# Order around the v, q and k products, weights loaded and combined in order of use, and the last projection in plain products

## The chip, the cores and the metric

The kernel runs on one core of one Trainium2 chip. The metric is device time in microseconds (us) of one execution; lower is better. Every run below was in the fast state, with a mean granted TensorE clock of 0.991 to 0.997 of full speed, so runs can be compared directly. "Span" is the time from the first to the last instruction in the profiled execution; it is about 1.8 us shorter than the timed run.

Engines are named as in the profile: PE is TensorE, PEld its weight loads, DVE is VectorE, ACT is ScalarE, POOL is GpSimd, SP is SyncE, which issues most transfers.

## The reference, cut to what matters

B = 32 batches, N = 512 nodes, D = 512 features, float32, one 0/1 adjacency matrix for all batches.

```python
# layer 0: graph step with residual and layer norm
deg = adj.sum(axis=1)
y   = deg[None, :, None] * (x @ Wi.T + b) + einsum('ij,bjo->bio', adj, x @ Wj.T)
h   = layernorm(x + y)
# layer 1: masked attention with 8 heads of 64, residual, layer norm
q, k, v = h @ Wq.T + bq, h @ Wk.T + bk, h @ Wv.T + bv       # split into heads
s   = where(adj == 0, -inf, q @ k.T / sqrt(64))
out = layernorm(h + (softmax(s) @ v) @ Wo.T + bo)
```

## The kernel before

**Seven pieces for one product.** Each 512 x 512 x 512 product of layer 0 (l0, two products in one), of v, q, k and of the output projection (pj) is made of seven half-size products ("pieces") of sums and differences of quarters, which fall into three PSUM groups. The weights' combinations are made once ahead of the loop and stored to HBM; they come back 256 KB at a time through a ring of 12 tiles. The activations' combinations (`combos`) are made by GpSimd for every batch.

```python
GROUP = {1: "X", 2: "X", 6: "Y", 7: "Y", 4: "Y", 5: "Z", 3: "Z"}   # which PSUM group a piece adds to
ORDER = (1, 2, 6, 7, 4, 5, 3)

def mm_tile(bank):                       # two banks, "a" and "b", one buffer each
    return psum.tile([P, 512], FT, name="mm" + bank, bufs=1)
def big():
    return work([P, 4, N], "big", 6)     # six large tiles in rotation

def piece(kind, b, i, bank):
    g = GROUP[i]
    ...                                  # eight matmuls (16 for l0) into the group's bank
    if i == 1:
        nc.scalar.copy(p1, pm)           # ScalarE keeps piece 1; the group goes on in the same bank
    ...                                  # kind v: piece 2 copied by ScalarE, others added by VectorE
    ...                                  # kind q, k: piece 2 emptied by ScalarE, others by VectorE
```

Whatever follows into a bank must wait until the bank is read. The order around v, q and k was:

```python
def phase_c(n):                          # norm[i]: turn 128 normed rows with PE, copy with ScalarE
    res = [norm[0], norm[1], z(apply, n, 1), z(add_bo, n, 0), pc("v", n, 1, "a")]
    ...
    res += [pc("q", n, 1, "b"), pc("v", n, 2, "a"), pc("q", n, 2, "b")]
    ...
    res += [norm[2], z(combos, TH, n, h, (1, 2), 0), pc("k", n, 1, "a"), norm[3], z(combos, TH, n, h, (1, 2), 1),
            z(combos, TH, n, h, (3, 4), 0), z(combos, TH, n, h, (3, 4), 1), z(add_bo, n, 1), pc("k", n, 2, "a")]
    ...
    for i in ORDER[2:]:
        res += [pc("v", n, i, "a"), pc("q", n, i, "b")]
```

**The start.** Six weights are loaded from two queues, and their combinations made, all ahead of the first product. So is the fold of v's bias into the output bias, a small matmul over wo, which stands before the combination of wo.

```python
def combine(name, eng):
    s1, s2, s3, s4, n22 = [ring_tile() for _ in range(5)]
    eng.tensor_tensor(s1, a21, a22, op=OP.add)
    eng.tensor_tensor(s2, s1, a11, op=OP.subtract)
    eng.tensor_tensor(s4, a12, s2, op=OP.subtract)
    eng.tensor_tensor(s3, a11, a21, op=OP.subtract)
    nc.scalar.mul(n22, a22, -1.0)
    ...                                  # seven 256 KB stores to HBM, two of them plain quarters

combine("wj", nc.gpsimd); combine("wi", nc.vector)
...                                      # graph forms: edge, the check of the adjacency (buffer adj_f)
combine("wv", nc.gpsimd); combine("wq", nc.vector); combine("wk", nc.gpsimd)
...                                      # fold: bo_r += bv @ wo
combine("wo", nc.vector)
```

**The loop.** The attention of one batch has eight steps (four head pairs, two halves). Pieces of the neighbouring batches are dealt into the steps, and behind each piece one of the six VectorE steps left over from the head pair (four reciprocal quarters, a check that sums into `told`, the scaling). The last projection runs alone behind the last attention.

## Time and profile before

| | before |
|---|---|
| time, median of 3 runs | 4076.63 us (4075.16 to 4078.4) |
| span of the profiled run | 4072.7 us |
| first l0 product starts | 62.0 us |
| first v piece starts | 88.69 us |
| one batch in the middle | 124.1 us |
| waits of PE between 150 and 3900 us | 109 us |
| from the last sums to the end | 41.1 us |

The prediction shows the totals, the waits and one period. To them belongs the longest of PE's waits in the first 150 us. Columns: who waits for whom, us in total, how often, the longest.

```profile
PE mmb L570 <- DVE big L569: 20.9, 1, 20.9
```

This is the fold (L570), which waits 20.9 us. What is behind it in PE's order waits with it: the rest of the gathering of the first batch begins only at 46.8 us, when the fold is done, and ends at 58.4. The first product then waits 3.6 us more for its weights, whose loads SyncE issues at 58.3, behind the last stores of wo.

### The profile page before, as it was taken

The numbers are of one execution on the slowest core, as the hardware profiler recorded it, in microseconds if no ns is written. First come the engines' busy times: TensorE is split into PE (matmuls) and PEld (weight loads), VectorE is DVE, ScalarE is ACT, GpSimd is POOL, SyncE is SP. The second block draws the span as 40 slices with busy tenths as digits, with TensorE's granted clock in tenths as the row PEclk, the third lists the DMA queues.
The fourth block names the chain that finished last, engine by engine and source line by source line (L and its number), as shares of the span: only waits on it lengthen the run. The fifth ranks groups of instructions, "written<-read, shape, count | busy, mean of one in ns | idle before, by whom it ended". The sixth has DMA issues, their size and how long they took to land.

```text
span 4072.7 us, 47394 instructions
## 1 busy us (share of the span) xinstructions
PE 3878.7 (95%) x17442; PEld 2655.8 (65%) x17442; DVE 2604.5 (64%) x3514; ACT 1058.0 (26%) x1486; POOL 1889.5 (46%) x2010
## 2 busy tenths in 40 slices
PE   6999999999999999999999999999999999999996
PEld 4766666666666666666666666666666666666663
DVE  3576666666666666666666666666666666666665
ACT  2222222222222222222222222222222222222221
POOL 5444544545445445345454454453454444444533
PEclk8999999999999999999999999999999999999998
DMA  8333333233333333332333333333333333333330
GB/s 286 104 99 106 107 111 117 86 114 104 103 120 98 104 106 107 109 118 88 110 109 102 118 99 101 109 109 106 117 98 102 110 103 114 105 95 114 104 101 24
DMA packets 239099, 441.49 MB, mean 108 GB/s; under 512 B 23440, under 2 KB 26512, under 8 KB 238864
## 3 DMA queue, kind: packets, MB, share of 16 engines
q1 hardware_dynamic: 237024, 434.73, 35.4%
q8 instruction: 142, 2.33, 0.2%
q10 hardware_dynamic: 1584, 3.15, 0.2%
q14 instruction: 93, 0.76, 0.1%
q0 software_dynamic: 256, 0.53, 0.0%
HBM read 393.75 MB, written 44.56 MB: 108 GB/s over the span
## 4 chain that ended last, share of the span: by engine, by line
PE 70%; DVE 17%; POOL 6%; issue 3%; ACT 3%; SPq 0%; DMA 0%; POOLq 0%; ACTq 0%; DVEq 0%
PE mma L342 28%; PE mmb L342 15%; PE sc L394 9%; PE ov L416 9%; PE mmb L266 6%; DVE xh L279 5%; DVE rl L429 3%; DVE e L399 3%; POOL big L311 2%; PE ov L423 2%; DVE es L408 2%; POOL mv L235 2%; ACT xh L239 2%; PE sc L259 1%; DVE ov L434 1%
## 5 line engine op out<-in xcount | busy, mean ns | idle before, releaser
L342 PE MATMUL mma<-ring,big 128*128 128x256 f32 x5296 | 1231.1, 382 | 73.3 <-POOL big L311 30.2
L342 PEld LDWEIGHTS mma<-ring,big 128*128 128x128 f32 x5296 | 993.0, 190 | 274.8 <-POOL big L311 41.8
L398 ACT ACTIVATE sc<-sc 128x1024 f32<-128x1024 f32 x512 | 492.9, 1007 | 1645.9 <-PE sc L394 1451.8
L399 DVE TENSOR_TENSOR e<-sc,edge 128x1024 f32<-128x1024 f32 x512 | 602.3, 1218 | 359.3 <-ACT sc L398 359.3
L311 POOL TENSOR_TENSOR big<-big 128x256 f32<-128x256 f32 (+1 forms) x512 | 541.9, 1083 | 289.3 <-DVE big L260 196.7
L405 POOL TENSOR_TENSOR es<-e 128x1024 f32<-128x1024 f32 x128 | 301.2, 2353 | 736.5 <-PE ov L423 699.9
L416 PE MATMUL ov<-e,v 128*64 128x512 f32 x2048 | 500.2, 610 | 26.1 <-DVE told L434 26.1
L394 PE MATMUL sc<-q,k 64*128 64x512 f32 x2048 | 509.6, 616 | 0.4 <-ACT big L288 0.4
L429 DVE RECIPROCAL rl<-ov 128x128 f32<-128x128 f32 x512 | 458.9, 927 | 4.0 <-PE ov L423 0.2
L342 PE MATMUL mma<-big,ring 128*128 128x256 f32 x1792 | 430.2, 383 | 24.2 <-ACT p L349 20.5
L234 POOL TENSOR_SCALAR mv<-mv 128x1 f32<-128x1 f32 x256 | 78.9, 308 | 774.8 <-DVE mv L233 762.0
L342 PE MATMUL mmb<-big,ring 128*128 128x256 f32 x1792 | 432.6, 384 | 0.0
L342 PEld LDWEIGHTS mmb<-big,ring 128*128 128x128 f32 x1792 | 333.1, 190 | 113.9 <-DVE e L399 47.9
L342 PEld LDWEIGHTS mma<-big,ring 128*128 128x128 f32 x1792 | 332.2, 190 | 103.2 <-ACT p L349 27.8
L416 PEld LDWEIGHTS ov<-e,v 128*64 128x64 f32 x2048 | 125.6, 137 | 370.8 <-issue 302.1
L408 DVE TENSOR_TENSOR es<-es,e 128x1024 f32<-128x1024 f32 x256 | 313.4, 1224 | 4.4
L394 PEld LDWEIGHTS sc<-q,k 64*128 64x128 f32 x2048 | 176.4, 186 | 207.8 <-issue 194.8
L360 DVE TENSOR_TENSOR xh<-xh,mma 128x512 f32<-128x512 f32 x192 | 131.7, 686 | 264.5 <-PE mma L342 264.5
L357 POOL TENSOR_TENSOR xh<-xh,p 128x512 f32<-128x512 f32 x192 | 237.9, 1267 | 105.8 <-ACT p L349 105.1
L342 PE MATMUL mmb<-ring,big 128*128 128x256 f32 x1104 | 270.2, 389 | 15.5 <-POOL big L311 15.5
L342 PEld LDWEIGHTS mmb<-ring,big 128*128 128x128 f32 x1104 | 206.6, 192 | 94.9 <-POOL big L311 40.3
L239 ACT ACTIVATE xh<-xh,mv 128x512 f32<-128x512 f32 x256 | 201.8, 813 | 255.5 <-POOL mv L236 255.1
(106 smaller groups left out, 3634.6 us busy)
## 6 DMA issues: line engine op xcount, KB each, us to landing
ring<-wi SPq DMA_DIRECT2D x224, 256.0 KB, 2.6
ring<-wj SPq DMA_DIRECT2D x224, 256.0 KB, 2.7
ring<-wv SPq DMA_DIRECT2D x224, 256.0 KB, 2.6
ring<-wq SPq DMA_DIRECT2D x224, 256.0 KB, 2.6
ring<-wk SPq DMA_DIRECT2D x224, 256.0 KB, 2.7
ring<-wo SPq DMA_DIRECT2D x224, 256.0 KB, 2.6
xh<-in_x_dram SPq DMA_DIRECT2D x32, 1024.0 KB, 5.5
out_dram<-xh SPq DMA_DIRECT2D x32, 1024.0 KB, 5.2
```

Of the source, the lines that this page charges most:

```text
L239: nc.scalar.activation(y, y, AF.Identity, bias=mv[:, 4:5], scale=mv[:, 3:4])
L266: nc.tensor.matmul(pm, parts[w][:, jc, :], adjR[:, jc, :], start=(w == 0 and jc == 0), stop=(w == 1 and jc == NC - 1))
L311: nc.gpsimd.tensor_tensor(dst, p, q, op=OP.subtract)
L342: nc.tensor.matmul(pm[:, c * Q:(c + 1) * Q], lhs, rhs, start=first, stop=(kc == 1 and n == len(terms) - 1), skip_group_check=True)
L357: nc.gpsimd.tensor_tensor(d, d, p1, op=OP.add)
L394: nc.tensor.matmul(ps[:, s, :], KT[b, hp // 2][r, hp % 2, kc * P:(kc + 1) * P], QT[b, hp // 2][r, hp % 2, :], start=True, stop=True)
L398: nc.scalar.activation(ps, ps, AF.Exp)
L399: nc.vector.tensor_tensor(e, ps, edge[:, kc:kc + 1, :].to_broadcast([P, 2, N]), op=OP.mult)
L405: nc.gpsimd.tensor_add(ES[hp], E[0], E[1])
L408: nc.vector.tensor_add(ES[hp], ES[hp], E[kc])
L416: nc.tensor.matmul(PV[hp][s * HD:(s + 1) * HD, :], V[b][:, kc, c0:c0 + HD], E[kc][:, s, :], start=(kc == 0), stop=(kc == NC - 1))
L429: nc.vector.reciprocal(rl[:, c], pl[:, c])
```

## The change

Its intent: fill the hole ahead of the second v piece, deal the leftovers of a head pair faster, start the first product as early as possible by loading and combining the weights in the order of their use, and keep the last projection from running alone. The diff, cut to its core:

```diff
@@ loads: adjacency in four chunks, then x and the weights on one queue @@
-    nc.sync.dma_start(adj_i, rows(adj))
+    for ic in range(NC):
+        nc.sync.dma_start(adj_i[:, ic, :], adj[ic * P:(ic + 1) * P, :])
@@ combine: tiles of a ring of four, two stores fewer @@
-        s1, s2, s3, s4, n22 = [ring_tile() for _ in range(5)]
+        s1, s2, s3, s4, n22 = [t[:, c].rearrange("p (c i) -> p c i", c=2)
+                               for t in [work([P, 2, N], "e", 4) for _ in range(3)] for c in range(2)][:5]
@@ query scale moves from wq into the Exp @@
-        nc.scalar.activation(ps, ps, AF.Exp)
+        nc.scalar.activation(ps, ps, AF.Exp, scale=QSCALE)
@@ phase_a: graph forms while the first batch is gathered @@
+            if n == 0 and i == 3:
+                res += [z(graph_forms)]
@@ phase_b: combinations of wv, wq, wk between the first l0 pieces @@
+                if n == 0:
+                    res += [z(combine, *f) for f in {6: (("wv", nc.vector),), 2: (("wq", nc.vector),),
+                                                     5: (("wk", nc.vector),)}.get(i, ())]
@@ phase_c @@
-        res = [norm[0], norm[1], z(apply, n, 1), z(add_bo, n, 0), pc("v", n, 1, "a")]
+        res = [z(fold)] if n == 0 else []            # fold: combine("wo"), then the bias product
+        res += [norm[0], norm[1], z(apply, n, 1), pc("v", n, 1, "a"), pc("q", n, 1, "b")]
...
-        res += [pc("q", n, 1, "b"), pc("v", n, 2, "a"), pc("q", n, 2, "b")]
...
-        res += [norm[2], z(combos, TH, n, h, (1, 2), 0), pc("k", n, 1, "a"), norm[3], ...
+        res += [norm[2], norm[3], z(combos, TH, n, h, (1, 2)), pc("v", n, 2, "a"), pc("q", n, 2, "b"),
+                pc("k", n, 1, "a"), z(combos, TH, n, h, (3, 4)), z(add_bo, n, 0), z(add_bo, n, 1), pc("k", n, 2, "a")]
@@ leftovers of a head pair: two behind an l0 piece @@
+                    some = ... else max(1, round(f[0] / PC))
@@ last steps: pieces of batch 30 packed two to a step, plain products of batch 31 @@
+        own = [(4 * GA, last_part, hp, 0) for hp in range(3)]
+        return [[z(last_load), p[0], FLUSH] + c, [p[1], p[2]], [p[3], p[4]], [p[5], p[6], z(stats, m, 0), z(stats, m, 1)],
+                [FLUSH, own[0], z(apply, m, 0), z(apply, m, 1), z(store, m)], [own[1]], [FLUSH, own[2]], []]
```

A `last_part(hp, half)` is four plain matmuls of one head pair for two row blocks. Half 0 of the first three pairs lies in the last attention; the other ten pairs of matmuls follow it.

## The prediction

> **What bounds the kernel now.** I read the totals first, then the waits of TensorE over the middle of the run (150 to 3900 us), then one period of a batch in order of time (2026 to 2075 us), and last the two ends.
>
> ```profile
> PE 3878.7 (95%) x17442; PEld 2655.8 (65%) x17442; DVE 2604.5 (64%) x3514; ACT 1058.0 (26%) x1486; POOL 1889.5 (46%) x2010
> ```
>
> TensorE (PE) sets the time; nothing else is over 65%. So the change can win only where PE stands still. The waits of PE in the middle, as total us, times, longest:
>
> ```profile
> PE mma L342 <- ACT p L349: 42.8, 59, 0.8
> PE mma L342 <- POOL big L311: 28.3, 29, 1.0
> PE ov L416 <- DVE told L434: 16.4, 31, 0.7
> PE mma L342 <- DVE v L368: 9.4, 29, 0.3
> ```
>
> With two smaller rows (6.9 and 5.2) this is 109 us, 2.7% of the run: a ceiling for the middle. One batch takes 124.1 us (the first l0 piece of one period starts at 1986.18, of the next at 2110.32). Start, duration, engine:
>
> ```profile
> 2032.49 0.14 DVE L434 DVE_READ_ACCUMULATOR2_ANT told<- 128x1 f32 x1
> ...
> 2032.68 1.94 PE L416 MATMUL ov<-e,v 128*64 128x512 f32 x8 [0.52 <-DVE told L434]
> ...
> 2040.82 0.81 ACT L239 ACTIVATE xh<-xh,mv 128x512 f32<-128x512 f32 x1 [2.02 <-POOL mv L236]
> ...
> 2041.54 0.56 ACT L349 COPY p<-mma 128x512 f32<-128x512 f32 x1
> ...
> 2042.16 1.99 PE L342 MATMUL mma<-ring,big 128*128 128x256 f32 x8 [0.78 <-ACT p L349]
> ...
> 2054.01 1.99 PE L342 MATMUL mma<-big,ring 128*128 128x256 f32 x8 [0.69 <-ACT p L349]
> ...
> 2056.04 0.84 ACT L382 ACTIVATE k<-mma,bk_c 128x256 f32<-128x256 f32 x2 [1.60 <-PE mma L342]
> 2056.98 1.97 PE L342 MATMUL mma<-ring,big 128*128 128x256 f32 x8 [0.97 <-POOL big L311]
> ```
>
> A piece that isn't stopped takes 1.73 us from start to start. Against that pitch the second v piece (2042.16) loses 0.94: ScalarE must first do a layer norm that itself waited for GpSimd, then copy the first v piece. The second k piece (2054.01) loses 0.86. The sixth v piece (2056.98) loses 1.24. It is put down to the GpSimd combination (L311), but the fourth of these, the one it needs, ended at 2056.56, whereas ScalarE emptied bank a of the second k piece until 2056.88, and PE started 0.10 us later. That is the same lag as behind other ScalarE releases. So I read this wait as the emptying of bank a. The values step loses 0.59 (2.51 from start to start where 1.92 is usual).
>
> The two ends:
>
> ```profile
> 40.17 6.77 PE L570 MATMUL mmb<-xh,big 128*128 128x512 f32 x8 [20.91 <-DVE big L569]
> ...
> 62.00 3.72 PE L342 MATMUL mma<-ring,big 128*128 128x256 f32 x16 [3.60 <-DMA ring<-wi]
> ```
>
> ```profile
> 4032.60 1.99 PE L342 MATMUL mma<-ring,oT 128*128 128x256 f32 x8
> 4045.15 3.78 PE L342 MATMUL mmb<-ring,big 128*128 128x256 f32 x8 [10.56 <-POOL big L311]
> ```
>
> The first real product starts at 62.0; the last projection runs alone, with a hole of 10.6 us.
>
> **What the Trainium skill says.** "TensorE: Matmul & The Clock Gate", What's actually happening: after an idle window of about 3.4 us the array runs at half its clock until it has been busy as long. The trace agrees: the granted clock is 0.50 from 24 to 40 us, and the values step after a wait of 3.05 us took 3.32 us instead of 1.94. "Perfetto Trace Analysis", Matmuls: independent groups should rotate through PSUM banks so that emptying one lies beside filling the next. The k2-to-v6 wait shows what happens without it. "DMA: Bandwidth & Descriptors", Issuing engines are not separate DMA queues: two issuing engines share the same 16 engines. That agrees: with both queues issuing by 1 us, wj and wi landed 12.0 and 16.9 us after issue. "ScalarE: Activation LUTs", What it computes: scale is part of the instruction, so the query scale in Exp should be free; no trace yet shows the Exp with it.
>
> **The change, part by part.**
>
> Around v, q and k. The last two turnings of the normed rows (0.43 us each on PE) move from beside q2 and k1 to before v2. They fill the hole there: v1 starts at 2037.66, q1 at 2039.49, the turnings then run from 2041.22 to 2042.1, and v2 may start at 2042.16 as before. The second turning needs the norm that ends at 2041.63, so about 0.05 of new wait: gain 0.94 - 0.05 = 0.89. But k1 and k2 now touch: k2 waits for ScalarE's copy of k1. The same pair at 96.12 and 98.74 in the first batch shows start to start 2.62, with ScalarE free, so the loss is 0.89, not the 0.86 of before. And v6 still follows k2 in the same bank a: its wait of 1.24 stays, although the combinations are now ready much earlier. Sum of this part: 0.89 - 0.03 = 0.86 us a period.
>
> Two leftovers per l0 piece. The reciprocal quarters, check and scaling of a head pair (six VectorE steps) were dealt one a piece; an l0 piece now takes two. In the step that matters the pieces are pj, l0, pj, l0: four steps dealt before, six now. So the check ends near 2030.97 + 0.75 = 2031.7, before PE is ready at 2032.09. Gain up to 0.59; I count 0.5, as the scaling behind it ends near 2032.4.
>
> Middle: 0.86 + 0.5 = 1.36 us, over 30 full periods 41 us. The first two periods about cancel (+0.9 for the second; the first loses 0.4, as it had no hole at v2). The two norms of the older batch move to after k2 and lie beside PE.
>
> The beginning. Removed: 12 stores of untouched quarters, four of the six combinations ahead of the first product, the scaling of wq, and the order mix-up of loads. Adjacency arrives alone (1 MB at the 350 GB/s of 4 to 8 us: near 5.5 instead of 10.7), so everything to the degrees comes 5 us earlier. But wj and wi now need six tiles from a ring of four. The third step of wi waits until stores of wj have landed, and these stand behind the nine 1 MB loads, which at this rate end near 30 us. I estimate VectorE held until 33 and the four gatherings until 42 to 45, so the first product near 43 instead of 62. Then VectorE is the limit: graph forms 1.2 + 2.3 + 2.3, base rows four times 1.25 to 1.7, then combinations of wv, wq, wk at 2.8 each; wq and wk also wait for the previous stores (about 3 us each). I get the last l0 piece ending near 76 (before: 86.3), then wo (2.8) and the fold of the bias, which used to run in the idle start and now stands on the path: a wait of some 5 us and 3.5 us of products, up to 7 at half clock. So v1 starts near 87 instead of 88.7. Gain 2 us, uncertain by 8.
>
> The end. The projection of the last batch becomes plain products: 16 of 0.86 us = 13.8 us instead of 7 x 1.73 = 12.1, but six of them lie inside the last attention. After the last sums (4031.6) before needs 41 us: scaling, four combinations, seven pieces, norm, a 1 MB store. After: six products 5.2 (the reciprocals, 3.4, hide under them), four more 3.4, row work on VectorE 4 x 1.56 = 6.2, the last row's GpSimd and ScalarE 2.2, a 256 KB store 3.3, end 1.7: 22 us, or 25 with a cold PE. In exchange the last attention gets longer: the pieces of batch 30 are packed two to a step into the first half, and the third part waits for its own scaling ahead of the last scores. I estimate 6 us lost. Gain 19 - 3 - 6 = 10 us.
>
> Sum: 41 + 0.5 + 2 + 10 = 53.5; 4076.6 - 53.5 = 4023.
>
> **The rivals.** First: the wait of v6 is GpSimd, as the profile names it. Then 1.24 us more a period, 37 us in all, and 3986. For it: the named releaser, and the diff's aim to have the combinations ready sooner. Against it: the 0.10 us lag behind ScalarE and 0.41 behind GpSimd, and the first batch, where v6 started at 101.71 just behind ScalarE's 101.61. Second: the start is as good as meant, with no tile wait, the l0 pieces ending near 62 and v1 near 72: 15 us more, 4008. Against it: the ring of four tiles. Third: new waits eat the middle's gain: the check and scaling of the second head pair now follow pieces that VectorE empties (norms no longer count among the six pieces of that step), leaving 0.4 us to spare, and x is loaded a pair of pieces later. It has some 10 us for a load of 5.5. If half the gain goes, 4044. Fourth, VectorE becomes the bound: at 64% no, except in the first 80 us and in the last attention.
>
> **Range and chances.** The middle is worth 41 with an error of 8, the start 2 with 8, the end 10 with 6: together about 13, so 17 for 8 in 10 if I have the waits right; I widen below for the first two rivals: 3996 to 4046. Faster by over 2% means below 3997: 0.12. Within 2%: 0.87. Slower: 0.01.
>
> **What would show it.** The row of v waits on ScalarE's copy should fall from 59 to about 30, the one on L434 nearly go, but a wait of about 1.0 before v6 should stay, now named after ScalarE's k (L382). The period should be near 122.8 us. The first l0 product should start near 43, the first v piece near 87, with a wait of PE at the fold. After the last sums some 22 to 25 us should remain. I am wrong if v6 starts at once behind k2, if the period is under 122 or over 123.6, or if v1 starts before 80.

## The result and the profile after

The changed kernel takes 4022.84 us (median of 4 runs, 4020.67 to 4023.47) against 4076.74 us for the kernel before in the same rounds. The ratio is 0.9867, with a 95% interval of 0.985 to 0.9884. Ratios here are the mean time of one kernel's fast runs over the mean of the other's in the same rounds, so not quite the ratio of the medians quoted. That is 1.3% faster. The prediction said 4023. One batch in the middle takes 122.5 us instead of 124.1 (predicted: near 122.8).

Cutting both traces at the same two events, the first v piece of the first batch and the scores of step 0 of the last batch, shows where the 51.0 us of span went:

| stretch | before | after | gained | predicted |
|---|---|---|---|---|
| start to the first v piece | 88.7 | 94.5 | -5.8 | +2 (with 8 of error) |
| first v piece to the last attention | 3872.1 | 3827.3 | +44.8 | +41.5 |
| last attention to the end | 111.9 | 99.9 | +12.0 | +10 |
| sum | 4072.7 | 4021.7 | +51.0 | +53.5 |

The middle and the end each gained 2 to 3 us more than predicted, and the start lost where it was to gain a little. The total came out close because these errors have opposite signs.

The middle itself can be cut at the first l0 piece of each batch (138.9, 248.1 and 3848.1 us before; 145.1, 256.6 and 3810.1 after). The 29 periods between the last two cuts gain 1.60 us each, 46.5 in all, and what follows them gains 1.0. What is ahead of them loses 2.7: 0.4 in the first batch, as predicted, and 2.3 in the second, where the prediction had a gain of 0.9. There the two turnings, which now come earlier, wait 1.6 us for VectorE; no later batch has this wait.

The totals of the changed kernel, as busy time, share and instructions, are hardly different; it is PE's idle time that shrank:

```profile
PE 3876.8 (96%) x17418; PEld 2655.3 (66%) x17418; DVE 2608.9 (65%) x3524; ACT 1059.7 (26%) x1483; POOL 1851.6 (46%) x1866
```

PE's waits in the middle (150 to 3850 us) of the changed kernel:

```profile
PE mma L356 <- issue: 28.3, 29, 1.0
PE mma L356 <- ACT p L363: 20.3, 30, 0.7
PE mma L356 <- DVE v L382: 9.4, 29, 0.3
...
PE ov L430 <- DVE told L448: 0.7, 1, 0.7
```

All lines of code moved by 14 (L342 is now L356, L349 is L363, L434 is L448). The wait on the copy of piece 1 fell from 59 times to 30, the wait on the check from 30 to 1 (31 up to 3900 us). The 28.3 us of the sixth v piece are there unchanged to the tenth, only their name is another: "GpSimd combination" has become "issue". The same stretch of one period in order of time (start, duration, engine, line):

```profile
2026.46 1.04 PE L301 MATMUL sc<-ident,xh 128*128 128x128 f32 x8
...
2027.33 1.97 PE L356 MATMUL mma<-ring,big 128*128 128x256 f32 x8
...
2028.79 2.60 POOL L325 TENSOR_TENSOR big<-big 128x512 f32<-128x512 f32 x2 [0.27 <-ACT big L302]
...
2038.27 1.99 PE L356 MATMUL mma<-big,ring 128*128 128x256 f32 x8 [0.68 <-ACT p L363]
...
2040.30 0.84 ACT L396 ACTIVATE k<-mma,bk_c 128x256 f32<-128x256 f32 x2 [2.08 <-PE mma L356]
...
2041.24 1.97 PE L356 MATMUL mma<-ring,big 128*128 128x256 f32 x8 [0.97 <-issue]
```

The two turnings (L301) now stand ahead of the second v piece (2027.33), which doesn't wait. The second k piece (2038.27) waits for the copy of the first, as predicted. The sixth v piece (2041.24) starts 0.10 us after ScalarE has emptied the bank (2041.14). The two combinations of the normed rows that come first (2028.79), the second of which it needs, had ended at 2031.39.

The start of the changed kernel:

```profile
34.87 0.69 DVE L217 TENSOR_TENSOR e<-big,e 128x512 f32<-128x512 f32 x1 [12.23 <-DMA wj<-e]
...
46.02 3.62 PE L356 MATMUL mma<-ring,big 128*128 128x256 f32 x16
...
49.14 11.83 POOL L325 TENSOR_TENSOR big<-big 128x512 f32<-128x512 f32 x7 [4.99 <-DVE told L198]
...
52.66 6.61 PE L356 MATMUL mmb<-ring,big 128*128 128x256 f32 x16 [3.02 <-POOL big L325]
...
65.51 5.32 PE L356 MATMUL mmb<-ring,big 128*128 128x256 f32 x16 [2.79 <-DVE xh L374]
...
86.69 6.64 PE L560 MATMUL mmb<-xh,big 128*128 128x512 f32 x8 [5.51 <-DVE big L559]
...
94.50 2.00 PE L356 MATMUL mma<-ring,big 128*128 128x256 f32 x8 [0.29 <-ACT big L302]
```

The first line is VectorE waiting 12 us until stores of wj have left the tiles it needs. The first l0 product starts at 46.0 instead of 62.0. But from there on PE stops three times, and after each stop it runs at half its clock for a while (granted 0.50 from 52.6, from 65.5 and from 86.6 us): 6.61, 5.32 and 6.64 us for work that takes about 3.6 us at full clock. The first stop is GpSimd (L325) waiting for VectorE to finish the graph forms (L198): these work in the buffer of the adjacency, which is one of the six large tiles in rotation and is the one that GpSimd needs next. The second is VectorE itself, and the third the fold.

Why VectorE was late in the second stop shows in its own instructions. First two steps of a combination with a GpSimd step beside them, then one without:

```profile
58.09 1.75 DVE L215 TENSOR_TENSOR e<-v 128x512 f32<-128x512 f32 x1
...
59.26 1.71 POOL L325 TENSOR_TENSOR big<-big 128x512 f32<-128x512 f32 x1
59.87 1.64 DVE L216 TENSOR_TENSOR e<-e,v 128x512 f32<-128x512 f32 x1
...
66.56 0.69 DVE L216 TENSOR_TENSOR e<-e,v 128x512 f32<-128x512 f32 x1
```

A step of 0.69 us takes 1.64 to 1.75 us while GpSimd works on tensors in SBUF, and GpSimd's takes 1.7 instead of 1.26. The Trainium skill, "SBUF — State Buffer", Who interferes with whom, says that a VectorE instruction with two inputs in SBUF contends with a GpSimd instruction that reads SBUF, since its second input comes through a read port that the two share. These lines agree: both become slower.

The end of the changed kernel:

```profile
3988.73 2.07 PE L599 MATMUL mma<-xh,oT 128*128 128x512 f32 x2 [4.83 <-DVE oT L453]
...
4000.27 1.08 PE L437 MATMUL ov<-es,ones 128*64 128x512 f32 x4 [1.31 <-DVE es L422]
4001.28 5.42 PE L599 MATMUL sc<-xh,oT 128*128 128x512 f32 x12
```

From the last sums (4000.27) to the end only 21.4 us are left, instead of 41.1. In exchange the last attention, from its first scores to its last sums, takes 78.5 us instead of 70.8. The third part of the plain products (3988.73) waits 4.83 us for the scaling of its own head pair, ahead of the last scores, which are then slower too (2.80 us at 3992.44, instead of 1.99).

### The profile page after: what moved, and what is told of

Its sections match the earlier page's. It is cut to its first block, busy times and chain, and to the rows that moved or that the text cites. A ratio compares the mean times of both kernels' runs of the same rounds, so it can differ in the third digit from the quotient of the medians.

```text
span 4021.7 us, 47158 instructions
## 1 busy us (share of the span) xinstructions
PE 3876.8 (96%) x17418; PEld 2655.3 (66%) x17418; DVE 2608.9 (65%) x3524; ACT 1059.7 (26%) x1483; POOL 1851.6 (46%) x1866
## 4 chain that ended last, share of the span: by engine, by line
PE 81%; DVE 14%; issue 3%; ACT 1%; POOL 1%; DMA 0%; SPq 0%; POOLq 0%; ACTq 0%; DVEq 0%
PE mma L356 32%; PE mmb L356 17%; PE sc L408 10%; PE ov L430 10%; PE mmb L280 6%; DVE xh L293 5%; DVE rl L443 3%; PE ov L437 2%; DVE es L422 2%; DVE e L413 2%; PE sc L273 1%; PE sc L301 1%; DVE ov L448 1%; ACT big L302 0%; ACT p L363 0%
## 5 line engine op out<-in xcount | busy, mean ns | idle before, releaser
L356 PE MATMUL mma<-ring,big 128*128 128x256 f32 x5288 | 1228.1, 382 | 47.3 <-issue 29.3
L356 PEld LDWEIGHTS mma<-ring,big 128*128 128x128 f32 x5288 | 991.6, 190 | 236.4 <-issue 66.3
L412 ACT ACTIVATE sc<-sc 128x1024 f32<-128x1024 f32 x512 | 492.8, 1006 | 1563.2 <-PE sc L408 1562.1
L325 POOL TENSOR_TENSOR big<-big 128x512 f32<-128x512 f32 x384 | 525.0, 1390 | 236.5 <-DVE big L274 196.8
L356 PE MATMUL mma<-big,ring 128*128 128x256 f32 x1792 | 430.2, 383 | 24.6 <-ACT p L363 20.9
L356 PE MATMUL mmb<-big,ring 128*128 128x256 f32 x1792 | 432.6, 384 | 0.0
L356 PEld LDWEIGHTS mmb<-big,ring 128*128 128x128 f32 x1792 | 333.1, 190 | 113.9 <-issue 47.9
L356 PEld LDWEIGHTS mma<-big,ring 128*128 128x128 f32 x1792 | 334.8, 190 | 110.5 <-ACT p L363 33.4
L356 PE MATMUL mmb<-ring,big 128*128 128x256 f32 x1080 | 267.3, 392 | 10.7 <-POOL big L325 8.0
L183 POOL TENSOR_TENSOR xlo<-xh,xhi 128x512 fp32r<-128x512 f32 x128 | 162.6, 1281 | 220.8 <-ACT xhi L182 220.7
L356 PEld LDWEIGHTS mmb<-ring,big 128*128 128x128 f32 x1080 | 203.9, 194 | 90.7 <-POOL big L325 33.1
```

Of the source, the lines that this page charges most:

```text
L325: nc.gpsimd.tensor_tensor(dst, p, q, op=OP.subtract)
L356: nc.tensor.matmul(pm[:, c * Q:(c + 1) * Q], lhs, rhs, start=first, stop=(kc == 1 and n == len(terms) - 1), skip_group_check=True)
L412: nc.scalar.activation(ps, ps, AF.Exp, scale=QSCALE)
```

## The experiments

All kernels gave correct results. Times are medians of 4 or 5 fast runs; the kernel before was timed in the same rounds each time (its medians lie between 4074.3 and 4076.7, so differences of 1 or 2 us between rounds mean nothing). Gains "less" than the changed kernel are differences of medians unless said otherwise; by the ratios, s1, s2 and s3 gain 6, 7 and 8 us. Where I compare spans, the first v piece of kernels with the same start scatters between 93.6 and 94.9 us, so single spans are good to about 1 us.

### a1_order_undone: the order around v, q and k as before

```diff
-        res += [norm[0], norm[1], z(apply, n, 1), pc("v", n, 1, "a"), pc("q", n, 1, "b")]
-        ...
+        res += [norm[0], norm[1], z(apply, n, 1), z(add_bo, n, 0), pc("v", n, 1, "a")]
+        ...                              # and all the rest of phase_c as in the kernel before
```

> The changed kernel, with the old order around v, q and k (turnings beside q2 and k1, combinations in halves, add of bo and norms of the older batch where they were). My theory: the hole before v2 (0.94 us a period against the pitch of 1.73) comes back, the waits before k2 and v6 stay: 30 periods by 0.96 = +29 us, near 4052 us. Rival, that the two leftovers per l0 piece made all of the middle's gain: near 4023.

Measured: 4044.68 us, ratio 0.9923 (0.9906 to 0.9939). The order is worth 22 us, some 7 us less than I expected. That isn't the period: with the old order it is 123.42 us long instead of 122.53, so the order is worth 0.89 a period, as predicted (0.86). Over 29 periods that is some 26 us. Of these 2.3 are lost again in the second batch, where the turnings wait for VectorE, and about 1 is hidden by the start, which came earlier in the trace of this run. The rival (no part of the gain) falls. The wait on the copy of piece 1 is back at 59 times and 40.0 us, and the 28.3 us carry GpSimd's name again. So the profile changes the name of that wait with the order, though its size is the same.

### a2_one_leftover: one leftover behind an l0 piece

```diff
-                    some = 0 if f[0] == 0.0 else len(extra) if step == 0 else max(1, round(f[0] / PC))
+                    some = 0 if f[0] == 0.0 else len(extra) if step == 0 else 1
```

> The changed kernel, with one leftover step per piece again. My theory: the values step waits for the check (L448) again, 0.59 us a period by 30 = +18 us, near 4041 us. Rival, that the order around v, q and k alone made the gain: near 4023.

Measured: 4042.09 us, ratio 0.9916 (0.99 to 0.9933), as expected. The wait on the check is back with 15.8 us in 30 waits. The period is 123.22 us, 0.69 longer. One edit of a few characters carries 19 us.

### a3_banks: the sixth v piece no longer follows k into its bank

Group Y and Z of k go to bank b, the gathering to bank a, and q stands before v in the later pairs, so that the sixth v piece no longer follows the second k piece into bank a (k's second piece still waits for the copy of its first).

```diff
-        k = [pc("k", n - 1, i, "a") for i in ORDER[2:]] if n > 0 else []
+        k = [pc("k", n - 1, i, "b" if n < B else "a") for i in ORDER[2:]] if n > 0 else []
@@ l0_gather @@
-        pm = mm_tile("b")
+        pm = mm_tile("a")
@@ phase_c @@
-            res += [pc("v", n, i, "a"), pc("q", n, i, "b")]
+            res += [pc("q", n, i, "b"), pc("v", n, i, "a")]
```

> The changed kernel, with q before v in the later pairs, k6 to k3 in bank b and the gathering in bank a, so that no two pieces of the same bank touch at k2-v6 or v3-k6; the combinations are untouched and q6 needs the same one as v6. My theory, that v6 waits for ScalarE to empty bank a of k2: the loss of 1.24 us a period goes, 31 by 1.24 = -38 us, near 3985 us. Rival, that the piece waits for the GpSimd combination: the wait moves to q6 and the time stays near 4023 us.

Measured: 3991.08 us, ratio 0.9791 (0.9775 to 0.9807; against the line of 2% that is "unclear"). The second largest wait of PE in the middle, behind that for the copy of piece 1 (20.3 us, as in the changed kernel):

```profile
PE mmb L356 <- DVE q L399: 15.2, 30, 0.5
```

The row of 28.3 us is gone, under either name. The combinations are made as before, and the sixth q piece, which now stands there and needs the same one, doesn't wait, so it was the bank. Of the 38 us expected 32 came: a wait of 0.3 us on VectorE in each period has become one of 0.5 (9.4 us have become 15.2).

### a4_interleaved: the same for the second k piece

The sixth q piece, in bank b, goes between the first and second k piece, so that the copy of k's piece 1 lies beside it. From then on q runs one piece ahead of v.

```diff
-                pc("k", n, 1, "a"), z(combos, TH, n, h, (3, 4)), ..., pc("k", n, 2, "a")]
+                pc("k", n, 1, "a"), z(combos, TH, n, h, (3, 4)), ..., pc("q", n, 6, "b"), pc("k", n, 2, "a")]
-        for i in ORDER[2:]:
-            res += [pc("v", n, i, "a"), pc("q", n, i, "b")]
+        for i, j in zip((7, 4, 5, 3, None), ORDER[2:]):
+            res += [pc("q", n, i, "b")] if i else []
+            res += [pc("v", n, j, "a")]
```

> As the run with the banks, and q6 set between k1 and k2 with q one piece ahead of v from there on, so that v5 and v3 are parted by the scores of the next step. My theory: the loss before k2 (0.84 us) goes as well: 31 by 2.08 = -64 us, near 3959 us. Rival, that ScalarE or GpSimd is too late for the denser order (the combinations for q7 come after k1): half of the gain, near 3990 us.

Measured: 3964.90 us, ratio 0.9728 (0.9711 to 0.9744). The largest wait of PE that is left in the middle:

```profile
PE mma L356 <- DVE v L382: 15.2, 30, 0.5
```

The middle's two large waits are both gone, and 58 us with them. This kernel beats both.

### s0_all_ahead: the start's work ahead of the first product again

Graph forms, all combinations (in tiles of the large ring) and the fold come before the first product, as in the kernel before, but with the new loads and with fewer stores.

```diff
-        res = [z(fold)] if n == 0 else []
+        res = []                                     # likewise graph_forms and combine in phase_a, phase_b
+    graph_forms()
+    combine("wv", nc.gpsimd); combine("wq", nc.vector); combine("wk", nc.gpsimd)
+    fold()
```

> The changed kernel with its new loads, but all six combinations, the graph forms and the fold of the bias ahead of the first product again, in tiles of the ring. My theory: the start lost (first v piece at 94.5 us against 88.7 before) because the deferred work stands on VectorE's path between the l0 pieces. Without it the first product comes later (near 55 us, behind 30 stores), but then runs through: v1 near 82 us, total near 4010 us. Rival, that deferring is good and only the loads or the clock hurt: v1 at 95 us or later, 4023 us or more.

Measured: 4019.48 us, ratio 0.9861 (0.9846 to 0.9876): 3 us better where I expected 13. The start of this kernel:

```profile
46.19 6.20 PE L558 MATMUL mmb<-xh,big 128*128 128x512 f32 x8 [28.90 <-DVE big L557]
...
63.66 3.62 PE L360 MATMUL mma<-ring,big 128*128 128x256 f32 x16
```

My expectation missed that the fold is also first in PE's order: the gathering of the first batch stood behind it until 52. From 63.66 on the l0 pieces run nearly without a stop (one wait of 0.17 us), and the first v piece comes at 90.7. So the deferral brings the first product forward by 18 us (63.7 to 46.0), and yet the first v piece comes 4 us later. That isn't the deferral alone, since this kernel has the larger ring of tiles, too; with larger tiles for wi and everything still deferred (next run) the first v piece comes at 87.6. So deferred work is worth 3 us, if its tiles don't wait.

### s1_wi_in_ring: no wait of VectorE for the stores of wj

```diff
+        if name == "wi":
+            s1, s2, s3, s4, n22 = [ring_tile() for _ in range(5)]
+        else: ...                                    # the ring of four, as in the changed kernel
```

> The changed kernel with the combinations of wi in ring tiles, so that they wait for no store of wj. My theory: VectorE is not held until 34.9 us and ScalarE not until 35.5, the gathering ends near 33 instead of 46 us, the first product starts near 37, and all behind it comes 9 to 11 us earlier: v1 near 84, total near 4012 us. Rival, that the stores bound the first product anyway: it stays near 45 and the total near 4022.

Measured: 4015.77 us, ratio 0.9852 (0.9837 to 0.9867), 7 us less. The first product starts at 39.3 instead of 46.0 and the first v piece at 87.6 instead of 94.5. So the wait that the ring of four causes is on the path with 7 us, and no more: stops behind it stay (2.0, 3.2 and 6.0 us).

### s2_fold_later: the fold's product behind the first k piece

The combination of wo and the forms of bv stay where the fold was; only the eight matmuls and the addition go behind the first k piece.

```diff
-        res = [z(fold)] if n == 0 else []
+        res = [z(fold_forms)] if n == 0 else []
...
-                pc("k", n, 1, "a"), z(combos, TH, n, h, (3, 4)), z(add_bo, n, 0), ...
+                pc("k", n, 1, "a"), z(combos, TH, n, h, (3, 4)), z(fold_sum), z(add_bo, n, 0), ...   # n == 0
```

> The changed kernel with the products of the fold moved behind k1 of the first batch; its VectorE part stays. My theory: the wait of 5.5 us and the half clock of the fold (6.6 instead of 3.5 us) go, 8 us in all: v1 near 83, total near 4015 us. Rival, that the norm of the rows is as late as the fold: under 3 us gained.

Measured: 4014.37 us, ratio 0.9849 (0.9836 to 0.9863), 8.5 us less. The fold in its new place:

```profile
92.16 3.60 PE L567 MATMUL mmb<-xh,big 128*128 128x512 f32 x8
```

It waits for nothing and runs at full clock, 3.60 us instead of 5.51 of wait and 6.64. These two differences are 8.55 us, which is the gain within the scatter (8.5 by the medians, 7 by the ratios, 9 by the spans).

### s3_graph_early: graph forms ahead of the first combinations

```diff
-            if n == 0 and i == 3:
-                res += [z(graph_forms)]
...
+    graph_forms()
     combine("wj", nc.gpsimd)
     combine("wi", nc.vector)
```

> The changed kernel with the graph forms (three VectorE passes and the edge table, 7 us as measured) ahead of the combinations of wi, where VectorE stands idle. My theory: in the changed kernel they hold the base rows and, since GpSimd's second combination reuses the buffer they read, also GpSimd until 49.1; without them both start 5 to 7 us earlier: v1 near 88, total near 4017 us. Rival, that the start is bound by GpSimd's port conflicts with VectorE alone: under 2 us gained.

Measured: 4013.05 us, ratio 0.9848 (0.9834 to 0.9861), 10 us less; I had expected 6. The first product starts 0.5 us earlier only (45.5), but the next two follow at 48.97 and 52.42 without a stop, and the two stops on VectorE behind them are 1.6 and 1.0 us, behind which the pieces take 3.72 us, so the clock didn't fall. The first v piece comes at 85.1. The edit does two things at once: it takes away GpSimd's wait for the tile, and it takes the 7 us of graph forms out of VectorE's way between the gathering and the l0 pieces. This run doesn't part the two.

### s4_one_load: the adjacency in one load again

```diff
-    for ic in range(NC):
-        nc.sync.dma_start(adj_i[:, ic, :], adj[ic * P:(ic + 1) * P, :])
+    nc.sync.dma_start(adj_i, rows(adj))
...                                                  # one cast instead of four
```

> The changed kernel with the adjacency in one load and one cast again (one part of the change undone; it still goes first on the one queue). If the prediction is right that the adjacency's way is 5 us shorter only because it comes alone and first, the cast starts near 6 and the degrees are no later than in the changed kernel, whose third and fourth chunk were cast only at 10.0 and 11.0. If the two late chunks come from the split itself (four issues, other loads between them), the one cast starts well before 10. If they come from loads sharing the engines, the cast starts near 10 again. In every case VectorE is held later by the stores of wj until about 35, so v1 stays near 94.5 and the time near 4023 (within 2 us). Rival: these 5 us are on the path of the start, and v1 moves by as much as the cast does.

Measured: 4020.80 us, ratio 0.9865 (0.9848 to 0.9881): no difference that the rounds could show. In the trace, though, the split is the wrong way round. The one cast of this kernel, and below it the first two and the last of the four casts of the changed kernel:

```profile
6.48 1.23 DVE L147 CAST big<-big 128x2048 f32<-128x2048 int32 x1 [6.48 <-DMA big<-in_adj_dram]
```

```profile
3.55 1.32 DVE L149 CAST big<-big 128x512 f32<-128x512 int32 x2 [3.55 <-DMA big<-in_adj_dram]
...
10.99 0.43 DVE L149 CAST big<-big 128x512 f32<-128x512 int32 x1 [0.52 <-DMA big<-in_adj_dram]
```

With the split two quarters are there early, but the last comes 3.7 us after a single load would have been cast to the end (11.42 against 7.71). Four issues take SyncE 1.82 us where one takes 0.45, and the traffic drops to 61 to 130 GB/s between 4.2 and 5.4 us. What holds the third and the fourth chunk so long stays open. In this one trace everything that follows was 2.3 us earlier (first product 43.7, first v piece 92.1), of which about 1 us may be scatter: in eight traces with the split and the same start, the first product lies between 45.0 and 47.0. So my expectation for this run, that VectorE's wait for the stores hides it, doesn't quite hold: those stores come earlier too. The rounds are too coarse to confirm 2 us.

### t1_third_part_later: the third part behind the last attention

```diff
-                [FLUSH, own[0], ...], [own[1]], [FLUSH, own[2]], []]
+                [FLUSH, own[0], ...], [own[1]], [FLUSH], []]
     for hp in range(HP - 1):
         last_part(hp, 1)
+    last_part(HP - 2, 0)
```

> The changed kernel with one part of the last projection (the two plain products of the third head pair for the first two row blocks, with the wait for their own scaling) moved from before the last scores to behind the last attention. If the 7.7 us that the last attention of the changed kernel lost are in part this wait and the cold array after it, the wait of 4.83 us on the scaling of oT goes, the last sums come about 5 us earlier, 1.7 us of products are added behind them, and the time is near 4020 (3 us less). Rival: the loss lies in the batch-30 pieces packed two to a step alone, and the wait only moves to another row: 4023, no change.

Measured: 4017.59 us, ratio 0.9859 (0.9844 to 0.9874), 3 us less by the ratios and 5.7 by the spans. The end of this kernel:

```profile
3987.63 3.79 PE L430 MATMUL ov<-e,v 128*64 128x512 f32 x16 [2.46 <-DVE told L448]
3992.74 1.08 PE L437 MATMUL ov<-es,ones 128*64 128x512 f32 x4 [1.31 <-DVE es L422]
```

The wait of 4.83 us is gone, and one of 2.46 us on the check, which it had hidden, is there instead. The last sums come 7.5 us earlier, and 23.3 us follow them instead of 21.4. So some 7 of the 10 us that the plain products add to the last attention (next run) are this one part: its wait, its matmuls at half clock and the scores behind them.

### t2_pieces_again: the last projection in seven pieces, alone

```diff
-                [FLUSH, own[0], z(apply, m, 0), ...], [own[1]], [FLUSH, own[2]], []]
+                [FLUSH, z(apply, m, 0), ...], [], [FLUSH], []]
+    run(TAIL[0])                          # seven pieces, stats, apply, one store, as in the kernel before
+    for g in rest(B - 1, HP - 1):
+        g[0](*g[1:])
+    for f in TAIL[1:]:
+        run(f)
```

> The changed kernel with the projection of the last batch in seven pieces again, alone behind the last attention with its combinations, statistics, norm and one store of 1 MB, and no plain products. If the plain products are what gained at the end (predicted: 19 us less behind the last sums against some 6 us longer in the attention), then behind the last sums some 40 us are found instead of 21.4, the last attention is some 5 us shorter, and the time is near 4037. Rival: the end's gain comes from how batch 30's pieces are dealt, and the form of the last projection is worth nothing: 4023.

Measured: 4029.44 us, ratio 0.989 (0.9874 to 0.9905), 9 us more than the changed kernel by the ratios and 5.9 by the spans; I had expected 14.

```profile
3989.74 1.06 PE L437 MATMUL ov<-es,ones 128*64 128x512 f32 x4
...
3999.75 3.78 PE L356 MATMUL mmb<-ring,big 128*128 128x256 f32 x8 [7.02 <-POOL big L325]
```

Behind the last sums 37.9 us follow (before: 41.1, as its hole was 10.6 us and is 7.0 here); the last sums come 10.5 us earlier than in the changed kernel. So plain products save 16.5 us behind and cost 10.5 in front. With the third part moved (t1) they save 14.6 and cost 3.

### best: everything together

a4, s1, s2, s3 and t1 in one kernel (not s4).

> All that was found put together: banks and the interleaved order of v, q and k as in a4 (3964.9 by itself), the combinations of wi in ring tiles, graph forms ahead of the first combinations, the product of the bias fold behind k1 with bank b free, and the third part of the last projection behind the last attention. If the gains of the start add up with the rest (first v piece near 74 instead of 94.5, the fold a few us later), the time is near 3942, ratio 0.967. If the gains of the start overlap (each takes away the same wait of VectorE), only some 10 us of them are seen: 3952. Over 3960 would say that the parts work against each other.

Measured: 3939.84 us (median of 5, 3939.14 to 3941.74), ratio 0.967 (0.9657 to 0.9683). The parts nearly add up: at the first v piece s1, s2 and s3 alone gave 6.9, 12.0 and 9.4 us, 28.3 in sum, and together they give 24.1. Three lines of its start, the first l0 product, the first v piece and the fold:

```profile
40.67 3.72 PE L360 MATMUL mma<-ring,big 128*128 128x256 f32 x16 [0.68 <-ACT big L290]
...
70.39 1.99 PE L360 MATMUL mma<-ring,big 128*128 128x256 f32 x8 [0.33 <-ACT big L306]
...
80.00 3.60 PE L570 MATMUL mmb<-xh,big 128*128 128x512 f32 x8
```

The first v piece is at 70.4 instead of 94.5, with the fold's 3.45 us (3.60 less the usual overlap) behind it: 20.6 us net, and t1's 5 at the end. From a4's 3964.9 that gives 3939.

## Why the prediction was right or wrong

**What bounds the kernel.** Right. PE is at 96%, and every us gained is one of PE's idle time.

**Order around v, q and k: right in the period, off in the second batch.** Each of its three steps came: no wait ahead of the second v piece, 0.84 lost at the second k piece against the usual pitch (predicted 0.89), and the sixth v piece waiting as before. Predicted 0.86 a period; undoing it cost 0.89 a period, but only 22 us in all (a1), since the second batch loses 2.3 us where the prediction had a gain of 0.9: the turnings' wait for VectorE there was not foreseen.

**Two leftovers per l0 piece: right.** I counted 0.5 a period (15 us); the run that undoes it says 0.69 (19 us in all). From scores to values 1.92 us pass now, the usual pitch, so the full 0.59 was gained; the prediction held back a tenth for nothing.

Order and leftovers make 0.89 + 0.69 = 1.58 of the 1.60 us found in each period, so nothing of size is left for a third cause there.

**First rival, GpSimd before the sixth v piece: rightly rejected.** The named releaser did not fit the ends of the two candidates in the trace, and the 0.10 us lag did. In the changed kernel the combinations were there 10 us early and the wait was still 28.3 us; with other banks (a3) it went. That the profile now writes "issue" and not, as I said, ScalarE's emptying of k is a miss in the naming only. The scale inside the Exp costs nothing, as the prediction concluded from the formula in the skill: 1007 ns before, 1006 ns after.

**The start: this is the step that failed.** The prediction said "v1 starts near 87 instead of 88.7. Gain 2 us, uncertain by 8". It came at 94.5: a loss of 5.8, at the edge of that margin and with the wrong sign. The mechanism was seen (tile wait, then VectorE as the limit, then the fold on the path), but three terms of the sum were too small, and one was too large:

- The first product, "near 43", came at 46.0. The adjacency was in at 11 instead of "near 5.5", because of the split into four (s4, about 2 us).
- From the first product to the end of the last l0 piece the prediction has 33 us (43 to 76); it took 35.2 (46.0 to 81.2), of which seven pieces at full clock are 24.2. The term "combinations of wv, wq, wk at 2.8 each" nearly held for the second and third, but the one of wv took 6.8 us (58.09 to 64.86), because GpSimd was working beside it. And it wasn't seen that GpSimd itself must wait for the graph forms, since they use a tile of its ring: 3.0 us, followed by a piece at half clock (3.0 more). s3 removes this wait together with the graph forms' own 7 us on VectorE: 9.4 us earlier at the first v piece.
- The fold: "a wait of some 5 us and 3.5 us of products, up to 7 at half clock". It was 5.5 and 6.6, so its worst case, some 2 us more than the middle that I used. Moved away (s2) it gives back 7 to 9 us.
- Too large: the waits of the combinations of wq and wk for the previous stores, "about 3 us each". They came to 0.46 us for wq and none for wk, which hid a part of the other misses.

The second rival, a start as good as meant, with v1 near 72, was rightly held to be unlikely for the change as it stands. Near 72 came only with further edits, the fold behind the first k piece among them: 70.4 in the run with everything together.

**The end: right in both halves.** Predicted 22 to 25 us behind the last sums: 21.4. Predicted 6 us lost in the last attention: 7.7. t2 shows that without the plain products the end would still have gained a few us over the kernel before, from how batch 30's pieces are dealt and a shorter hole; I had put all of the gain down to the products.

**Third rival, new waits in the middle: rightly given little.** x arrives in time and no new row of more than 2 us shows up.

**The total** was right to 0.2 us, by luck within the sum: -7.8 at the start against +3.3 in the middle and +2 at the end leave -2.5, and the two profiled spans happen to differ by 51.0 where the medians differ by 53.9.

## What to carry to other kernels

A wait's named releaser is only the last event that the profile saw: compare the end times of all that the instruction needs, buffers and PSUM banks too, and change the bank, or the order around it, before you change the engine (here 58 us, more than the whole change gave). Work taken from ahead of the first product and put among the first products isn't gone: ask which engine does it, who shares a port or a buffer ring with it, and whether PE's stop is long enough to halve the clock. Products which wait for their own input belong at the end of an engine's order, not in front of work that is ready.

## What the Trainium skill lacked or had wrong

- "SBUF — State Buffer", Who interferes with whom: it calls the shared ports an exclusive lock, and says of VectorE's two-port modes that the other engine is blocked for the whole instruction; for a step with two inputs in SBUF it says only that it contends, without durations. Here a 128 x 512 step takes 0.69 us on VectorE and 1.26 us on GpSimd alone; side by side each takes 1.64 to 1.75 us, so one of each in 1.7 us, less than the 1.95 us of one after the other.
- "TensorE: Matmul & The Clock Gate", What's actually happening: its table has the clock fall after at least one idle window of about 3.4 us. In the changed kernel it fell after less: the values step at 3956.46 had waited 2.24 us and took 3.62 us, at a granted clock of 0.50. After the same wait of 2.24 us in t2 it took 1.94 us. The page also says that the window runs freely, so that the moment of the change varies, and with that the runs agree: after a wait of 3.23 us an l0 piece took 6.59 us (s1), after 3.48 us 3.72 us (s2). In these runs a wait of 2.2 to 3.5 us may or may not halve the clock, so a prediction can only give chances.
- "DMA: Bandwidth & Descriptors", Bandwidth: its advice is to keep transfers at 1 MiB or more. No number is there for the split of one load that others follow: four of 256 KB were cast to the end at 11.42 us, one of 1 MB at 7.71 us, and four issues took 1.82 us of the queue's engine against 0.45.
- No page that I found: which releaser the profile names when a PSUM bank and a tensor come free close together. The same 28.3 us went under GpSimd's combination, then under "issue", and belonged to ScalarE's emptying of a bank.
